# A fused attention and feed-forward block: first token chunks prepared ahead of the branch, the feed-forward part's first work placed in the last KV head's turns

## The chip, the cores and the metric

The kernel runs on one core of a Trainium2 chip. The metric is the device time of one execution in microseconds (us). The core has a matrix engine (TensorE, PE in the profile), a vector engine (VectorE, DVE), an activation engine (ScalarE, ACT), a general engine (GpSimd, POOL) and SyncE (SP), which issues all DMAs here. Each engine executes its own list of instructions in order and waits on semaphores for the others. PEld is the loading of TensorE's weights.

## The reference

The inputs are 2 sequences of 1024 tokens, 512 wide, in float32. First comes an attention with two parts on the same projections, then a gated feed-forward whose weights are rounded to 16 levels (NF4). Both are wrapped in a layer norm before and after:

```python
x = x + layernorm(attn(layernorm(x), Wq, Wk, Wv, Wo))
x = x + layernorm(ffn(layernorm(x), w1, w2, w3))

def attn(h):                       # 32 query heads, 8 KV heads, D = 128, window W = 64
    q, k, v = h @ Wq, h @ Wk, h @ Wv
    g = k
    o_lin = gla_scan(softmax(q), softmax(k), v, log_sigmoid(g) / 16)
    y = sliding_window_attn(rope(q), rope(k), v)
    return bf16(0.5 * y + 0.5 * o_lin) @ Wo

def gla_scan(q, k, v, g):          # per token
    S = S * exp(g)[:, None] + k[:, None] * v[None, :]
    o = q @ S

def ffn(h):                        # 512 -> 1376 -> 512
    a, b, c = nf4(w1), nf4(w2), nf4(w3)      # absmax per 64 values, nearest of 16 codes
    return (silu(h @ a.T) * (h @ b.T)) @ c.T
```

## The kernel before

**Start.** All of `Wk` is loaded in four rows of 128x1024, squared on ScalarE, and summed by TensorE into the column norms (`norms`). From their largest value VectorE makes a flag, `small_gates` (line 1179). Every engine reads it and branches (`tc.If`, line 1181): `fast_attention` where a chunked form of the scan is safe in float32, else `general_attention`. Each is followed by `feed_forward`. These inputs take the fast branch.

**Tokens.** The 2048 tokens are 16 chunks of 128. `input_norms(ci)` loads a chunk into a quantisation tile (tag `zx`), `normed` normalises it on VectorE, with one POOL instruction (`rstd`, line 152, a power) inside it. `input_transposes(ci)` transposes it on TensorE in four 128x128 pieces and ScalarE copies the result into `xnT` (line 303). Four chunks are done ahead of the first turn; the others follow two per turn in turns 0 to 5.

**Turns.** The attention is a list of `N_` = 128 turns, one for each KV head `g`, sequence `b` and chunk `c`; a turn handles the four query heads of its KV head for 128 tokens. The calls of the turn's loop are written out by hand, apart for even and odd turns, and the engines get them in that order (`InOrder`, line 116, so nearly all attention instructions have that line in the profile). A turn works on three stages at once: scores, softmax, linear part and values of turn n; the projection of turn n - 1 by `Wo` (`project`, tile `py`), collected into `yacc` on VectorE; and the query products of turn n + 1. In even turns the key products (`pk`) of the two turns n + 2 and n + 3 are made as well. POOL does the rotary embedding of keys and queries (`rope`: `tmp`, `kr`, `qtmp`, `qr`).

**Weights.** `load_weights(g)` loads `wkv`, `wq` (two buffers each) and `wo` (one). `part_weights` splits `wo` on POOL into a rounded part and a remainder, `wop`, in a format TensorE takes faster: one cast and one subtraction for each of four heads. For head 0 it is called four times ahead of the first turn; for the others in turns 2 to 5 of the second sequence of the head before.

**Quantisation.** The rounding of `w1`, `w2` and `w3` runs as a list of steps (`order`) in all turns from `BEGIN` = 6 on: signs on ScalarE, a multiply-and-maximum chain on VectorE (`zp`, `zm`), six steps in an even turn and three in an odd one. The results go to DRAM (`dq1`, `dq2`, `dq3`).

**Feed-forward.** It begins when the attention's pools are closed. `tokens(x2T, ci)` normalises a chunk of `yacc`, adds the input, stores the sum in `yacc`, normalises again, and transposes into `x2T` (line 1115); `up_weights(f)` loads two rows of `dq1` and `dq2` and transposes them (`tw`, line 1089); `down_weights(f)` the same for `dq3` (line 1098). There are four blocks of 512 tokens and `NFT` = 11 rows of up to 128 hidden values. For every block and row TensorE makes `pgate` and `pup` (line 1136, four products of 128x128x512 each, two passes each), ScalarE the sigmoid (a table of its own), VectorE two multiplications into `hT`; then four output products `pf` per block (line 1154), a layer norm, the sum with `yacc` and the store. In the first block the weights are transposed two rows ahead of their use. A scheduler decides the order of this part's instructions.

## Time and profile before

| | us |
|---|---|
| median of 3 runs | 2175.61 |
| lowest and highest run | 2174.6, 2177.53 |
| profiled execution | 2172.86 |
| its span, first to last instruction | 2171.1 |
| TensorE busy | 2104.6 |
| flag ready on VectorE | 15.97 |
| first key product | 39.30 |
| first scores (`ps`) | 55.90 |
| last projection (`py`) begins | 1666.35 |
| first gate product | 1690.90 |

The mean granted TensorE clock is 0.988. A line of the profile's groups or timeline names line, engine, operation, the written tile, the read tiles, the shape, and how often it stands there; in a timeline the first two numbers are start and duration in us, and the brackets hold the idle time of the engine before it and what ended it. A matmul in float32 shows as two passes, so eight instructions for four products. Matmuls are pipelined: a single one shows as longer than the distance to the next.

### The profile page before, as it was taken

What the parts mean: (1) busy time and instruction counts of PE and PEld (TensorE: products, weight loads), DVE (VectorE), ACT (ScalarE), POOL (GpSimd) and SP (SyncE); (2) the same over time, 40 slices, a digit from 0 to 9 for tenths busy, and PEclk for the clock granted to TensorE, in tenths of its full rate; (3) what the DMA queues carried; (4) which work ended last, traced back from release to release, by engine and by line L of the source; (5) the groups of instructions that cost most, each with busy time, mean ns of one, the idle gap of its engine ahead of it and who ended that gap; (6) DMA issues with size and microseconds to landing.
All of it is one profiled execution on the core that took longest, in us unless ns stands there. A gap on an engine that the chain in (4) does not pass through costs nothing.

```text
span 2171.1 us, 27563 instructions
## 1 busy us (share of the span) xinstructions
PE 2104.6 (97%) x8948; PEld 1409.9 (65%) x8948; DVE 1489.6 (69%) x2822; ACT 1362.9 (63%) x3944; POOL 944.1 (43%) x1290
## 2 busy tenths in 40 slices
PE   4999999999999999999999999999996999999998
PEld 2667777777777777777777777777774544444443
DVE  3668888888788888888888888888887425142222
ACT  2568888888888888888888888888884210101000
POOL 3445555655475556456555655565452101010000
PEclk7999999999999999999999999999998999999999
DMA  5100100010010001000100100000002301000000
GB/s 194 45 15 11 59 11 15 25 49 11 9 58 10 15 15 59 11 10 20 53 11 15 39 33 11 12 11 20 13 6 68 115 27 39 0 29 0 20 0 21
DMA packets 45192, 64.52 MB, mean 30 GB/s; under 512 B 3632, under 2 KB 19632, under 8 KB 45040
## 3 DMA queue, kind: packets, MB, share of 16 engines
q1 hardware_dynamic: 45040, 62.67, 8.8%
q8 instruction: 73, 1.20, 0.2%
q14 instruction: 79, 0.65, 0.1%
HBM read 50.01 MB, written 12.65 MB: 29 GB/s over the span
## 4 chain that ended last, share of the span: by engine, by line
PE 90%; POOL 3%; ACT 2%; DVE 2%; DMA 1%; issue 1%; POOLq 0%; ACTq 0%; SPq 0%; DVEq 0%
PE pq L116 19%; PE py L116 10%; PE pk L116 10%; PE ot L116 9%; PE pgate L1136 7%; PE pf L1154 7%; PE pup L1136 7%; PE pa L116 7%; PE ps L116 5%; PE tr L116 3%; PE tq L116 3%; PE pg L116 2%; POOL qr L116 1%; PE pS L116 1%; PE pt L116 1%; ACT ps L116 1%
## 5 line engine op out<-in xcount | busy, mean ns | idle before, releaser
L116 PE MATMUL pq<-wq,xnT 128*128 128x512 f32 x1024 | 460.6, 592 | 0.0
L116 POOL TENSOR_TENSOR qtmp<-q,fcos 128x512 f32<-128x512 f32 x128 | 162.0, 1266 | 580.3 <-ACT q L116 580.3
L116 PEld LDWEIGHTS pq<-wq,xnT 128*128 128x128 f32 x1024 | 184.9, 190 | 183.7 <-issue 183.6
L116 ACT ACTIVATE zs<-xw,fbounds 128x512 bf16<-128x512 f32 (+3 forms) x416 | 287.8, 723 | 0.0
L116 PE MATMUL py<-wop,oc 128*128 128x512 f32 x1024 | 270.5, 406 | 1.3 <-ACT oc L116 1.3
L152 POOL TENSOR_TENSOR rstd<-ve,mhalf 128x1 f32<-128x1 f32 x64 | 35.7, 565 | 515.0 <-DVE ve L150 499.0
L116 ACT ACTIVATE ps<-ps,nms 128x128 f32<-128x128 f32 x512 | 175.0, 342 | 110.7 <-DVE nms L116 94.7
L116 PE MATMUL pk<-wkv,xnT 128*128 128x256 f32 x1024 | 233.4, 381 | 0.0
L116 ACT ACTIVATE pq<-pq,nmq 128x128 f32<-128x128 f32 x512 | 175.1, 342 | 91.7 <-DVE nmq L116 79.2
L1139 ACT ACTIVATE sg<-pgate 128x512 f32<-128x512 f32 (+1 forms) x44 | 26.2, 597 | 324.9 <-PE pgate L1136 324.9
L116 PEld LDWEIGHTS pk<-wkv,xnT 128*128 128x128 f32 x1024 | 195.9, 191 | 47.0 <-issue 14.1
L116 PEld LDWEIGHTS py<-wop,oc 128*128 128x128 f32 x1024 | 182.9, 189 | 36.6 <-ACT oc L116 1.7
L116 POOL TENSOR_TENSOR qr<-q,fsin 128x256 f32<-128x256 f32 x256 | 206.0, 825 | 0.0
L116 DVE SCALAR_TENSOR_TENSOR zp<-zp,zs 128x512 f32<-128x512 f32 (+3 forms) x224 | 195.4, 872 | 9.4 <-ACT zs L116 5.0
L116 POOL TENSOR_TENSOR qr<-qr,qtmp 128x512 f32<-128x512 f32 x128 | 165.8, 1295 | 9.8
L116 DVE SCALAR_TENSOR_TENSOR zm<-zm,zs 128x512 f32<-128x512 f32 (+3 forms) x192 | 163.0, 849 | 5.7 <-ACT zs L116 3.0
L1136 PE MATMUL pgate<-x2T,w1T 128*128 128x512 f32 (+1 forms) x352 | 160.4, 594 | 0.0
L1136 PE MATMUL pup<-x2T,w2T 128*128 128x512 f32 (+1 forms) x352 | 158.2, 592 | 0.0
L116 DVE TENSOR_TENSOR ps<-ps,fwin 128x512 f32<-128x512 f32 x128 | 89.2, 697 | 96.3 <-PE ps L116 95.4
L1154 PE MATMUL pf<-w3T,hT 128*128 128x512 f32 (+1 forms) x352 | 151.8, 592 | 0.0
L116 PE MATMUL ps<-kT,qrT 128*128 128x128 f32 x1024 | 136.5, 276 | 0.2
L116 DVE TENSOR_REDUCE nmq<-pq 128x4 f32<-128x512 f32 x128 | 87.8, 686 | 59.4 <-ACT q L116 59.4
(125 smaller groups left out, 4078.9 us busy)
## 6 DMA issues: line engine op xcount, KB each, us to landing
wq<-in_L_attn_Wq_dram SPq DMA_DIRECT2D x8, 1024.0 KB, 6.1
wo<-in_L_attn_Wo_dram SPq DMA_DIRECT2D x8, 1024.0 KB, 5.1
xw<-in_L_ffn_w_dram SPq DMA_DIRECT2D x20, 256.0 KB, 2.6
dq<-zp SPq DMA_DIRECT2D x20, 256.0 KB, 2.0
row<-dq SPq DMA_DIRECT2D x20, 256.0 KB, 2.8
x<-_attn_hidden_states_dram SPq DMA_DIRECT2D x16, 256.0 KB, 2.7
xc<-_attn_hidden_states_dram SPq DMA_DIRECT2D x16, 256.0 KB, 2.6
out_dram<-res SPq DMA_DIRECT2D x16, 256.0 KB, 2.0
```

The source lines that it names most:

```text
L116: return lambda *args, **kwargs: self.tc.keep_in_program_order(getattr(self.engine, name)(*args, **kwargs))
L152: nc.gpsimd.tensor_tensor(rstd, ve, mhalf, ALU.pow)
L1136: nc.tensor.matmul(pg[:n, :], lhsT=wT[:, kt, f * P : f * P + n], rhs=x2T[:, kt, :], start=kt == 0, stop=kt == KT - 1)
L1139: nc.scalar.activation(sg[:n, :], ps[0][:n, :], AF.Sigmoid)
L1154: nc.tensor.matmul(pf, lhsT=hT[:n, f, m * P : (m + 1) * P], rhs=w3T[:n, f, :], start=f == 0, stop=f == NFT - 1)
```

## The change

1. **Ahead of the branch.** `xnT`, `wkvs`, `wqs`, `wos` and the rotary `tables` are tiles of the whole kernel now. The part before the branch loads chunks 0 and 1 between rows 1 and 2 of `Wk`, chunks 2 and 3 after row 3, then head 0's `wkv`, `wq` and the tables; it normalises, transposes and copies the four chunks (`AHEAD` = 4) in a fixed order between the squares and the flag. Chunk 3 is normalised after the flag.
2. **Other chunks.** They are staged in a buffer of the `wop` tile, normalised in place, two in turns 0 and 1 and one a turn after that, in turns 2 to 9. `wo` of head 0 is loaded after the branch, and its parts are made after the first softmax transposes (two heads) and at the end of turn 0 (two heads). Quantisation begins with turn 2.
3. **Last KV head (turns 112 to 127).** `feed_forward_begun(n)` runs at the end of every turn. From turn 116 on it loads the first rows of the up weights, from turn 117 to 124 it transposes eight of them, one a turn; in turns 117, 119, 121, 123 it does the first half of a token chunk (`tokens`), in 118, 120, 122, 124 the second normalisation, in 119, 121, 123, 125 the transposes. Turn 126 makes the gate product of row 0, turn 127 the up product of row 0 and the gate product of row 1, and the up product of row 1 lies ahead of the last projection.
4. **Tiles.** The feed-forward part has no pools of its own: its weights, hidden values and work tiles lie in `wqs`, `wkvs`, `wos`, `tables`, the `wop` buffers, `xnT` and, after the last turn, the attention's tiles; PSUM is that of the attention. All its TensorE, VectorE and ScalarE instructions are kept in program order.

The diff, cut to its core (the general branch and the plain feed-forward that follows it are left out):

```diff
-            for ci in range(2 * CB):
-                input_norms(ci)
-                input_transposes(ci)
-            weights = {0: load_weights(0)}
+            def all_weights(g):
+                return *load_weights(g), parts_tile(f"wop{g}"), load_out_weights(g)
+            for ci in range(AHEAD, AHEAD + 2):
+                chunk_loaded(staged(ci), ci)
...
+            weights = {0: (*first_weights, parts_tile("wop0"), load_out_weights(0))}
             qb = load_const("fbounds", [P, 16], F32, con["bounds"])
+            for ci in range(AHEAD + 2, AHEAD + 2 * GRP):
+                chunk_loaded(staged(ci), ci)
...
-            for h in range(GRP):
-                part_weights(0, h)
             key_products(0)
...
             softmax_transposes(0)
-
-            BEGIN = (NCI - 2 * CB) // 2
+            for h in range(2):
+                part_weights(0, h)
+            arriving = iter(range(AHEAD, NCI))
+            BEGIN = 2
+            L = N_ - NB * NCH
+            F = FeedForward((pmm, "mm"), (psc, "sc"), (ptr, "tr"), (po, "o"))
...
+            def feed_forward_begun(n):
+                if n == L + 2:
+                    up = quarters(parts_tile("wup"))
+                    for f in range(4):
+                        F.w1[f], F.w2[f] = up[:, f, :], up[:, 4 + f, :]
+                    F.xc, F.yn, F.xn, F.sg = ([wqs[0][:, j, :]] for j in range(4))
+                    F.rows = [wos[:, j, :] for j in range(4)]
...
+                k = n - (L + 5)
+                if 0 <= k < 8:
+                    F.up_weights(k % 2, k // 2, early["row", k])
+                if -1 <= k < 7:
+                    early["row", k + 1] = F.load_up((k + 1) % 2, (k + 1) // 2)
+                if k >= 2 and k % 2 == 0 and k // 2 - 1 < F.MB:
+                    F.token_transposes(k // 2 - 1, early["xn"])
+                if k >= 0 and k // 2 < F.MB:
+                    if k % 2 == 0:
+                        F.tokens(k // 2, early["xc"])
+                    else:
+                        early["xn"] = F.token_norms(k // 2)
+                if k >= -1 and k % 2 and (k + 1) // 2 < F.MB:
+                    early["xc"] = F.load_tokens((k + 1) // 2)
...
-                inputs = list(range(2 * CB + 2 * n, min(2 * CB + 2 * n + 2, NCI)))
+                inputs = list(islice(arriving, 2 if n < 2 else 1))
...
                     if keys2:
                         key_products(n + CB)
+                    else:
+                        gate0 = F.up_product(0, 0, 0)
...
+                    if n == 0:
+                        for h in range(2, GRP):
+                            part_weights(0, h)
                 else:
+                    if not more:
+                        up0 = F.up_product(1, 0, 0, "gate")
                     score_softmax(n)
+                    if not more:
+                        F.hidden(0, gate0, up0, F.sigmoid(0, gate0))
...
+                    else:
+                        gate1 = F.up_product(0, 0, 1)
+                        sg1 = F.sigmoid(1, gate1)
                     values(n)
...
             rounded_heads(N_ - 1)
+            up1 = F.up_product(1, 0, 1)
             project(N_ - 1)
+            F.hidden(1, gate1, up1, sg1)
             collect(N_ - 1)
...
+            F.run(2, 4)
...
+    class FeedForward:
...
+        def token_norms(self, ci):
+            xn = self.next("xn")
+            normed(xn, yacc[:, ci, :], self.vector)
+            return xn
...
+        def run(self, f0, ready):
...
+                for f in range(f0 if tb == 0 else 0, NFT):
+                    gate = self.up_product(0, tb, f)
+                    sg = self.sigmoid(f, gate)
+                    if row:
+                        self.up_weights(0, row[0], row[1][0])
+                    if tb == 0:
+                        col = next_down(col)
+                    up = self.up_product(1, tb, f)
+                    if row:
+                        self.up_weights(1, row[0], row[1][1])
+                        row = loaded_up(next(ups, None))
+                    self.hidden(f, gate, up, sg)
...
         for kt in range(KT):
             nc.sync.dma_start(wka[:, kt, :], wk[kt * P : (kt + 1) * P, :])
-            nc.scalar.activation(wka[:, kt, :], wka[:, kt, :], AF.Square)
+            if kt % 2:
+                for ci in (kt - 1, kt):
+                    chunk_loaded(chunks[ci], ci)
+        first_weights = load_weights(0)
+        load_tables("fcos", "fsin")
...
+        for ci in range(2):
+            normed(chunks[ci], chunks[ci], vector)
+        squares(0)
+        squares(1)
+        transposed(0)
+        squares(2)
+        transposed(1)
+        squares(3)
+        normed(chunks[2], chunks[2], vector)
...
+        normed(chunks[3], chunks[3], vector)
+        transposed(2)
+        transposed(3)
     flag = nc.values_load(small_gates, min_val=0, max_val=1, skip_runtime_bounds_check_because="the result of a comparison")
```

## The prediction

> **What bounds the kernel now.** I read the page first (busy shares, then the 40 slices), then TensorE's waits, busy time by stage, and last the instructions in order of time at both ends of the attention.
>
> ```profile
> span 2171.1 us, 27563 instructions
> ...
> PE 2104.6 (97%) x8948; PEld 1409.9 (65%) x8948; DVE 1489.6 (69%) x2822; ACT 1362.9 (63%) x3944; POOL 944.1 (43%) x1290
> ...
> PE   4999999999999999999999999999996999999998
> ...
> PEclk7999999999999999999999999999998999999999
> ```
>
> TensorE is the bound, and it stands still in three places only: the first slice, slice 31, and the tail. The stages show how much:
>
> ```profile
> 16.00:22.30 6.30, 0.00 (x0) 0.00 (x0) 2.40 (x8) 0.00 (x0) 1.73 (x4) 0.76 0.69 228
> 22.30:39.30 17.00, 3.91 (x16) 3.19 (x17) 6.08 (x11) 1.75 (x3) 8.47 (x10) 0.50 0.79 245
> 39.30:44.90 5.60, 5.60 (x18) 4.59 (x18) 1.46 (x4) 0.60 (x2) 0.55 (x1) 0.65 0.92 283
> 44.90:55.90 11.00, 6.81 (x25) 3.88 (x23) 6.11 (x17) 6.45 (x22) 9.11 (x18) 0.89 0.49 166
> 55.90:70.20 14.30, 13.34 (x64) 9.86 (x64) 7.09 (x15) 7.89 (x27) 7.79 (x13) 0.97 0.06 21
> ...
> 1650.10:1668.50 18.40, 13.54 (x65) 9.69 (x64) 10.48 (x17) 7.04 (x22) 3.59 (x4) 1.00 0.03 12
> 1668.50:1687.30 18.80, 3.29 (x12) 2.15 (x12) 14.54 (x38) 1.75 (x3) 4.66 (x8) 0.58 0.61 196
> 1687.30:1698.80 11.50, 11.46 (x38) 6.88 (x39) 9.96 (x24) 4.81 (x7) 2.33 (x4) 0.80 0.51 156
> 1698.80:2163.00 464.20, 464.20 (x1205) 211.96 (x1203) 134.10 (x256) 42.13 (x73) 18.80 (x34) 1.00 0.08 24
> ```
>
> Columns: stretch, length, busy time of PE, PEld, DVE, ACT, POOL, granted clock, DMA. From 16 to 39 us TensorE does 3.9 us of work; from 1668.5 to 1687.3 it does 3.3 us at clock 0.58. After 1698.8 it never waits, so nothing there can be gained. In order of time, the start:
>
> ```profile
> 5.67 8.70 PE L1173 MATMUL norms<-wka,ones 128*1 128x512 f32 x16 [5.67 <-ACT wka L1171]
> ...
> 19.17 0.48 SPq L312 DMA_DIRECT2D wo<-in_L_attn_Wo_dram  x1
> ...
> 29.36 0.61 POOL L116 CAST wop<-wo 128x512 fp32r<-128x512 f32 x1 [7.13 <-DMA wo<-in_L_attn_Wo_dram]
> ...
> 39.30 5.55 PE L116 MATMUL pk<-wkv,xnT 128*128 128x256 f32 x16
> ...
> 52.74 0.58 PE L116 MATMUL pt<-ident,kh 128*128 128x128 f32 x2 [3.81 <-DVE kh L116]
> ```
>
> The flag is ready at 15.97, SP issues at 16.68, and the first key product waits until 39.30.
>
> **Part 1, the start.** *Ahead of the branch.* The four rows of Wk land 1.26 us apart (512 KB each). Two token chunks (256 KB, 0.63 each) now lie before rows 2 and 3, which land near 8.2 and 9.5. The new order ties ScalarE to TensorE: the square of row 2 stands behind the copy of chunk 0's transposes, the square of row 3 behind chunk 1's. TensorE begins at 5.67 with passes 0.86 apart for 3.8 us, then 0.43: rows 0 and 1 to 10.8, transposes 0.44; copy 0.58 and square 1.06 to 13.0; four passes 1.72, transposes, copy, square to 16.95; last passes to 18.8 (14.37 before). Reductions 1.6: flag at 20.7, 4.7 later. Chunk 3 is normalised after that (DVE 0.69+0.18+0.14, POOL 0.55, DVE 0.55, with gaps 2.3) and TensorE transposes it before its own branch: 23.5. With the 0.7 that SP's branch took, the first key product starts at 24.3 instead of 39.3: 15.0 gained. No row shows a branch with the DMA queues full; between 0.7 again and a DMA's landing (2.7) on top, I take 0.7, SP's row.
>
> [...]
>
> *Chunk 0's chain.* TensorE has then been idle 3.8 us, so I leave the key product its 5.55 (after the 3.81 us wait above, four transposes took 1.09 to 1.12 against 0.60 at full clock). [...] Now the parts of Wo: before, POOL made all of them from 29.36 to 37.99, under the wait for tokens. Now wo is issued after the branch, behind two chunks and three constants (near 26.5; it lands after 5.1 at the median, 32), and POOL's order has cast 0.61, subtract 1.26, cast 0.61 between chunk 0's key rope (done near 33.7) and query rope, and another 1.26 inside it: 3.7 on the path. The rope's transposes come at 41.7 (53.52 before, 11.8 gained). VectorE has chunk 6's normalisation, waiting for POOL, before qs: scores(0) at 44.8 against 55.90, 11.1 gained.
>
> *Turns 0 to 9.* The statistics and normalisations of chunks 7 and 8 stand before the mask of turn 0, each waiting for POOL, which is making the last two parts: mask 2.2 late, and scores(1) at about 61.8 against 70.16, 8.4 gained. From scores(1) to scores(10) before took 121.7; work is four pairs of 25.18 (the spacing of 1607.48 and 1632.66), a turn of 11.4 and ten transposes of 0.44, 116.5. Part of the 5.2 between is the second chunk of a turn, whose transposes wait for the first one's copy:
>
> ```profile
> PE xtp L116 <- ACT xnT L303: 4.0, 6, 0.7
> ```
>
> Now only turns 0 and 1 have two chunks: I give back 3.0. Quantisation starts four turns earlier, where the input norms were; its work per turn is that of the steady turns, 0.2 us of idle in 50: nothing. **Start: 11.4 gained**; ends 4 (branch fetch, later wo) and 17 (15.0 with warm clock, no rope delay).
>
> **Part 2, the transition.** From 1650.1 to 1698.84 is 48.7 us. Work at full clock in it: the attention's rest 12.0, 16 token and 16 weight transposes 3.5, two products of 3.44: 22.4. So 26.3 are lost. Now four token chunks and eight weight tiles lie in turns 117 to 125, the four products of the first two rows in turns 126 and 127. In turn 127 by rows: scores 0.9, up product 3.44, linear 1.7 end at +6.1, while mask, maximum, exponentials, sw end at +5.4; the sigmoid's table load (1.28) lies beside that, hT at +7.9, A at +8.6 under the projection (to +8.4) and gate product (to +11.8); values, then up product 3.44 over the heads' two copies (1.24). Nothing waits. Before, this stretch waited for S 2.3, sw 0.7, oc 1.3.
>
> *What it costs.* Each token chunk adds two normalisations of 2.1 in order on VectorE, with a POOL round trip inside. The even turn's end has no room, the odd one's 1.6:
>
> ```profile
> 1594.81 0.70 DVE L116 TENSOR_TENSOR ps<-ps,fwin 128x512 f32<-128x512 f32 x1 [1.59 <-PE ps L116]
> ...
> 1607.73 0.76 DVE L116 SCALAR_TENSOR_TENSOR zp<-zm,zp 128x576 f32<-128x576 f32 x1
> ...
> 1608.58 0.70 DVE L116 TENSOR_TENSOR ps<-ps,fwin 128x512 f32<-128x512 f32 x1
> ```
>
> The first line is an odd turn's successor, the last an even one's: its mask starts as the quantisation step ends. So `token_norms` at the even ends makes the next mask late by 2.1 less one weight transpose, 1.6, and odd turns have nothing to spare (rope's transposes wait for POOL by 0.2 to 0.5 there): 1.6 in turns 119 and 121, 0.8 in the two after, where quantisation runs out (its 544 steps at nine a pair from turn 2 end at 122.9). `tokens` at the odd ends costs 0.9, inside the even turn's 2.8 between sw (ended 1600.42) and mix (1603.22). Where a turn has both a weight and a token transpose, three times, the second waits 0.68: 2.0. ScalarE's three copies a pair (1.8) fit its idle 4.6 of 25; without that the exponentials would be late by as much. SP's row and token loads are issued turns ahead, so a 2.8 landing is hidden; late, they would hold TensorE by what is missing. **Six lost** in all; ends 2 (all cover holds) and 15 (every one of eight token steps stops TensorE for its 2.1).
>
> **Part 3, the rest.** First two rows aside, the feed-forward keeps its products, transposes and copies, now in program order on TensorE, VectorE and ScalarE. Product pairs of 6.9 us cover a transpose's copy (0.59 to 0.69) and the loads (2.8 to 3.2) one row ahead: nothing; ends 0 and 5 (0.1 a row over 44). The tail's last normalisation and store stay.
>
> **Sum.** 2172.86 - 11.4 - 26.3 + 6.0 = 2141.2 against the profiled execution (span 2171.1 and 1.8 around it). The median of the runs, 2175.61, lies 2.75 higher, so 2144.
>
> **Rivals.**
> 1. *More of the start is gained.* POOL gets wo late enough to do query rope first, and TensorE stays warm: 17 at the start, 2 lost in the turns: 2172.86 - 17 - 26.3 + 2 + 2.75 = 2134. For it: 15.0 is gained up to the first product. Against: POOL's order is fixed, and 3.81 idle did cool the clock.
> 2. *The engines of the last head have no room,* or the start is given back by wo: 15 lost in the turns gives 2153; only 4 gained at the start gives 2151. For it: VectorE is busy 82 to 85 us in 100 there. Against: after turn 122 quantisation is gone.
> 3. *The work is not really woven in:* a load or a reused tile makes the transposes wait until the attention is over. Then the 26.3 stay, 2172.86 - 11.4 + 2.75 = 2164. Against: tiles of the seventh head's weights are free from turn 112, and row loads need only the first two dequantised matrices (374 of 544 steps, done by turn 86).
> 4. *Slower: the last head's turns fall to half clock.* One mechanism, in turns 117 to 127: token steps in VectorE's queue stop TensorE for over 3.8 us a turn, after which it runs its first 3.8 us at half rate (1.9 lost), 5.7 a turn, 63 in eleven: 2172.86 - 11.4 - 26.3 + 63 + 2.75 = 2201. It decides from 37.7 / 11 = 3.4 lost a turn. My steps give at most 1.6; TensorE's 2.31 wait in turn 127 of before did not cool it.
>
> **How the numbers follow.** Forecast (2137 to 2150) 0.56; rival 1 (2129 to 2137) 0.17; rival 2 (2150 to 2160) 0.19; rival 3 0.04; rival 4 0.04. The range 2131 to 2158 leaves out rivals 3 and 4 and the outer ends of 1 and 2, about 0.15. A change under 0.2% (4.4 us) can't be told from none on this kernel: slower 0.04, same 0.01, faster 0.95.
>
> **What would show it.** After: the flag near 20.7 and the first key product near 24; the rope's first transposes ended by POOL's query rope with a wop operation inside it; scores(1) near 62; from turn 117 small waits of TensorE, in odd turns for VectorE's sw or POOL's rope and for ScalarE's copies at the second transposes; no wait over 2 us between the last scores and the first gate product of row 2, with a granted clock of 1.00 throughout; feed-forward turns as before. Wrong would be: a first key product after 28 or before 20, a wait over 3 us in the last head, or a TensorE busy time that grew by more than the clock's share.

## The result and the profile after

The changed kernel takes 2147.59 us (median of 4 runs, 2147.42 to 2148.68) against 2176.26 us (4 runs, 2174.6 to 2177.53) for the kernel before on the same chip: a ratio of 0.9874, 95% interval 0.9862 to 0.9887, 28.7 us faster. The forecast was 2144 with a range of 2131 to 2158. The profiled execution took 2147.43 us, 25.4 less than the one of before; its span, busy times, slices of TensorE and granted clock from the page:

```profile
span 2145.6 us, 27553 instructions
...
PE 2103.7 (98%) x8948; PEld 1409.7 (66%) x8948; DVE 1492.3 (70%) x2822; ACT 1359.7 (63%) x3944; POOL 944.6 (44%) x1290
...
PE   6899999999999999999999999999999999999998
...
PEclk8999999999999999999999999999999999999999
```

The slice that held the transition (slice 31, a 6 before) is full, and the first one holds more (6 instead of 4); the second holds a little less (8 instead of 9). The same 8948 matmuls and nearly the same busy time (2104.6 before) fill a span 25.5 us shorter: the change removed standing still, not work. Busy time by stage (stretch, length, busy time and instructions of PE, PEld, DVE, ACT, POOL, granted clock, DMA share, GB/s):

```profile
0.00:23.90 23.90, 11.67 (x32) 3.23 (x33) 7.52 (x19) 7.06 (x8) 2.98 (x12) 0.97 0.73 241
...
28.60:44.80 16.20, 7.46 (x24) 4.01 (x24) 7.62 (x23) 6.55 (x22) 14.61 (x24) 0.73 0.89 301
44.80:65.00 20.20, 16.84 (x65) 11.99 (x64) 10.78 (x24) 7.84 (x27) 12.28 (x19) 0.79 0.16 55
65.00:78.70 13.70, 12.67 (x66) 9.05 (x65) 8.91 (x23) 8.49 (x27) 6.04 (x9) 1.00 0.12 36
78.70:96.40 17.70, 15.83 (x71) 11.53 (x70) 11.85 (x29) 10.63 (x33) 9.20 (x13) 0.94 0.09 30
1526.70:1663.90 137.20, 132.44 (x639) 95.34 (x638) 102.56 (x206) 94.53 (x290) 65.28 (x94) 1.00 0.09 28
1663.90:2145.60 481.70, 473.61 (x1236) 218.06 (x1234) 156.97 (x297) 45.74 (x83) 21.90 (x40) 1.00 0.08 25
```

The stretches end at marks: first key product 23.9, scores of turn 0 at 44.8, of turn 1 at 65.0, turn 2 at 78.7, turn 3 at 96.4, turn 117 at 1526.7, turn 127 at 1663.9. From there TensorE works until the last normalisation and store. In the start 8.7 us still pass without work between the first key product's end and scores(0), and then, in turn 0, at clock 0.79, 3.4 more; turn 2 loses 1.9.

Comparing the start of each turn's scores with before tells where the gain lies:

| turn's scores | before | after | earlier by |
|---|---|---|---|
| 0 | 55.90 | 44.83 | 11.07 |
| 1 | 70.16 | 64.98 | 5.18 |
| 2 | 83.71 | 78.71 | 5.00 |
| 3 | 99.42 | 96.36 | 3.06 |
| 6 | 141.68 | 134.85 | 6.83 |
| 10 | 191.88 | 186.54 | 5.34 |
| 117 | 1532.48 | 1526.70 | 5.78 |
| 127 | 1656.09 | 1663.86 | -7.77 |
| end | 2171.1 | 2145.6 | 25.5 |

The start is worth 5.3 us, not the 11.4 forecast. Turns 117 to 127 take 137.16 us against 123.61, 13.55 more. 8.7 of it is work that was moved there (eight weight and four token transposes of 0.44, one product of 3.44); the other 4.8 are what waits cost. These are all the waits there (what TensorE waited for in the stretch from 1526 to 1670; total, times, longest):

```profile
PE ptr L118 <- ACT wup L118: 2.0, 3, 0.7
PE pa L118 <- DVE S L118: 1.5, 2, 0.8
PE tr L118 <- POOL qr L118: 0.9, 2, 0.5
PE pa L118 <- DVE sw L118: 0.4, 2, 0.2
```

They too sum to 4.8, but that is partly chance. Before, the same turns held 1.2 us of waits, so by the brackets only 3.6 are new; and the stop in turn 119 cost more than its bracket says: the product behind the wait of 0.82 starts 1.42 after the one ahead of it, where the same two lie 0.43 apart in the kernel before, so that it lost 0.99.

From scores(127) to the end it takes 481.7 instead of 515.0. The 33.3 less, minus the 8.7 of work that left, are 24.6 gained, so that the transition as a whole gives 24.6 - 4.8 = 19.8 (forecast: 26.3 - 6.0 = 20.3). Its heart is turn 127, in order of time:

```profile
1663.86 1.06 PE L118 MATMUL ps<-kT,qrT 128*128 128x128 f32 x8
1664.75 3.60 PE L118 MATMUL pgate<-xnT,wup 128*128 128x512 f32 x8
1668.19 0.59 PE L118 MATMUL pa<-qh,kT 128*128 128x256 f32 x2
...
1672.22 3.59 PE L118 MATMUL pgate<-xnT,wup 128*128 128x512 f32 x8
```

(The products of the feed-forward part carry the names pgate and pup by turns; the trace names a buffer, not its use.) No line has a bracket with a wait: the product of 3.44 lies where before TensorE waited 2.3 for the state S, the next stands between projection and values.

### The profile page after: what moved, and what is told of

Read it like the earlier page. It is cut to its first block, busy times and chain, and to the rows that moved or that the text cites. A ratio compares the mean times of both kernels' runs of the same rounds, so it can differ in the third digit from the quotient of the medians.

```text
span 2145.6 us, 27553 instructions
## 1 busy us (share of the span) xinstructions
PE 2103.7 (98%) x8948; PEld 1409.7 (66%) x8948; DVE 1492.3 (70%) x2822; ACT 1359.7 (63%) x3944; POOL 944.6 (44%) x1290
## 4 chain that ended last, share of the span: by engine, by line
PE 87%; ACT 4%; DVE 4%; POOL 3%; issue 1%; DMA 0%; ACTq 0%; POOLq 0%; DVEq 0%
PE pq L118 18%; PE py L118 9%; PE ot L118 9%; PE pk L118 9%; PE pgate L118 7%; PE pout L118 7%; PE pup L118 7%; PE pa L118 7%; PE ps L118 5%; PE tr L118 3%; PE tq L118 2%; PE pg L118 2%; POOL qr L118 2%; ACT ps L118 1%; PE pt L118 1%; PE pS L118 1%
## 5 line engine op out<-in xcount | busy, mean ns | idle before, releaser
L118 POOL TENSOR_TENSOR qtmp<-q,tables 128x512 f32<-128x512 f32 x128 | 162.2, 1268 | 586.8 <-ACT q L118 586.6
L118 POOL TENSOR_TENSOR qr<-q,tables 128x256 f32<-128x256 f32 x256 | 206.2, 826 | 0.0
L118 PEld LDWEIGHTS ps<-kT,qrT 128*128 128x128 f32 x1024 | 126.1, 194 | 0.9 <-ACT qrT L118 0.6
L118 ACT ACTIVATE ffqrT<-pgate 128x512 f32<-128x512 f32 (+1 forms) x21 | 12.5, 597 | 176.3 <-PE pgate L118 176.3
L118 PE MATMUL ot<-qh,S 128*128 128x512 f32 x224 | 114.4, 592 | 0.0
L118 ACT ACTIVATE wq<-pgate 128x512 f32<-128x512 f32 (+1 forms) x23 | 13.7, 597 | 153.1 <-PE pgate L118 153.1
```

What stands on the lines that cost most here:

```text
L118: return lambda *args, **kwargs: self.tc.keep_in_program_order(getattr(self.engine, name)(*args, **kwargs))
```

## The experiments

Each edit is made to the changed kernel, alone where nothing else is said. The medians stand beside its 2147.59 us, and beside 2174.6 to 2176.0 for the kernel before, which ran on the same chip as each. That kernel's own median thus moves by 1.4 us, so a difference of one or two us between medians says little by itself; there the traces have to decide.

### 1. The weave taken out, and the start undone

First the weave: the first tokens, weights and products of the feed-forward part stand behind the attention again.

```diff
-                if 0 <= k < 8:
-                    F.up_weights(k % 2, k // 2, early["row", k])
...
-                    if k % 2 == 0:
-                        F.tokens(k // 2, early["xc"])
-                    else:
-                        early["xn"] = F.token_norms(k // 2)
...
-                        gate0 = F.up_product(0, 0, 0)
...
-                        up0 = F.up_product(1, 0, 0, "gate")
...
-                        gate1 = F.up_product(0, 0, 1)
...
-            up1 = F.up_product(1, 0, 1)
...
-            F.run(2, 4)
+            for ci in range(F.MB):
+                F.tokens(ci, F.load_tokens(ci))
+                F.token_transposes(ci, F.token_norms(ci))
+            for f in range(2):
+                for i in range(2):
+                    F.up_weights(i, f, F.load_up(i, f))
+            F.run(0, 2)
```

> The start stays as in the changed kernel; the feed-forward part's first tokens, its first rows' weights and their four products follow the attention again. Theory (the weave is worth the 26.3 us of waits lost after the last turn, less the waits it puts into turns 117 to 127, 4.8 by the trace of the changed kernel; about 20 in all): 2147.6 + 20 = 2167 to 2169, turns 117 to 127 back from 137.2 to about 124 us, and TensorE standing still for over 20 us after the last turn. Rival (part of the 28.7 us gained in all is the start's, more than the 5.3 that the turns show): the weave is worth 14 or less, 2162 or below.

Measured: 2172.13 us (10 runs, 2169.7 to 2174.54; ratio to before 0.9985, 0.9976 to 0.9995); the profiled execution's span is 2167.6, 22.0 longer than the changed kernel's. Scores(117) come at 1526.63, the same as with the weave; turns 117 to 127 take 122.68, and then TensorE waits four times, here the first three (start, duration, instruction, wait ahead of it in brackets):

```profile
1667.77 1.11 PE L118 MATMUL ptr<-ident,wq 128*128 128x128 f32 x4 [6.07 <-DVE wq L118]
1673.06 1.11 PE L118 MATMUL ptr<-ident,wq 128*128 128x128 f32 x4 [4.17 <-DVE wq L118]
1678.57 1.09 PE L118 MATMUL ptr<-ident,wq 128*128 128x128 f32 x4 [4.39 <-DVE wq L118]
```

Each token chunk's second normalisation is waited for by itself, 19.0 us in four waits; written one after the other, these steps make the rest after scores(127) 3.3 longer than in the kernel before (518.3 against 515.0). Taking off these 3.3 and adding the 0.9 by which turns 117 to 127 are shorter than before, the 22.0 become 19.6. By the traces, then, the weave is worth about 20 us against the old kernel, as the theory has it, and the rival's 14 or less is out. The theory's time was too low: 2172.13 lies above its 2167 to 2169. The 3.3 of this edit were not in it, and the medians lie 24.5 apart, 2.5 more than the profiled executions (the profiled one was the fastest of the ten); no trace shows where these 2.5 lie.

Then the start: the first four chunks, weights and tables behind the branch, Wo's parts ahead of the first key product.

```diff
-            for ci in range(AHEAD, AHEAD + 2):
+            for ci in range(AHEAD):
                 chunk_loaded(staged(ci), ci)
+            for ci in range(AHEAD):
+                input_norms(ci)
+                input_transposes(ci)
+            first_weights = load_weights(0)
+            first_out = load_out_weights(0)
+            load_tables("fcos", "fsin")
...
+            for h in range(GRP):
+                part_weights(0, h)
             key_products(0)
...
-        for ci in range(2):
-            normed(chunks[ci], chunks[ci], vector)
-        squares(0)
-        squares(1)
-        transposed(0)
...
+        for kt in range(KT):
+            squares(kt)
```

> Chunks 0 to 3, the first head's weights and the tables are loaded, normalised and transposed after the branch again, and Wo's parts are made before the first key product; the weave stays. Theory (the start has kept 5.3 of the 15.4 us by which its first key product is earlier): 2147.6 + 5.3 = 2153, scores(0) near 56 and scores(2) near 84. Rival (the start is worth the 11.4 forecast and the rest is lost somewhere else): 2159.

Measured: 2150.09 us (2148.23 to 2151.72), ratio to before 0.9881 (0.9865 to 0.9898), 2.5 us slower than the changed kernel. TensorE at the start:

```profile
25.17 3.79 PE L118 MATMUL xtp<-ident,tokens 128*128 128x128 f32 x16 [10.31 <-DMA wkv<-in_L_attn_Wv_dram]
28.76 4.58 PE L118 MATMUL pk<-wkv,xnT 128*128 128x256 f32 x16
```

The first key product comes at 28.76 although the chunks are loaded after the branch: 10.5 earlier than the 39.30 of before, in which the four chunks went through two buffers and their second pair was loaded behind Wo. So the changed queue of loads behind the branch gives two thirds of the 15.4 us, and preparing ahead of the branch 4.8. Scores(0) were expected near 56 and came at 47.24; scores(10) at 190.47, 3.9 later than in the changed kernel. What this edit takes back is 3.9 in the trace and 2.5 in the medians, less than the theory's 5.3; the rival's 11.4 is out. It is not the price of the branch alone: all of Wo's parts stand ahead of the key rope on POOL here, which starts at 38.08.

### 2. Where the missing six microseconds went

Three candidates at the start: Wo's parts on POOL; normalisations that VectorE takes early; the squares ahead of the branch. POOL in the changed kernel, in order of time:

```profile
39.40 1.25 POOL L118 TENSOR_TENSOR wop<-wos,wop 128x512 fp32r<-128x512 f32 x1
40.62 1.25 POOL L118 TENSOR_TENSOR qr<-qr,qtmp 128x512 f32<-128x512 f32 x1
...
47.32 0.72 POOL L161 TENSOR_TENSOR rstd<-ve,mhalf 128x1 f32<-128x1 f32 x1
...
56.15 1.26 POOL L118 TENSOR_TENSOR qr<-qr,qtmp 128x512 f32<-128x512 f32 x1
57.37 0.55 POOL L161 TENSOR_TENSOR rstd<-ve,mhalf 128x1 f32<-128x1 f32 x1
```

and VectorE:

```profile
48.08 0.55 DVE L166 TENSOR_SCALAR tokens<-tokens,mv,rstd 128x512 f32<-128x512 f32 x1 [0.35 <-POOL rstd L161]
48.66 0.70 DVE L118 TENSOR_TENSOR ps<-ps,fwin 128x512 f32<-128x512 f32 x1
...
57.95 0.94 DVE L166 TENSOR_SCALAR tokens<-tokens,mv,rstd 128x512 f32<-128x512 f32 x1 [2.96 <-POOL rstd L161]
...
59.01 0.69 DVE L118 TENSOR_TENSOR qs<-pq,rsq 128x512 f32<-128x512 f32 x1
```

Between the two halves of the query rope stands a subtraction of Wo's parts (39.40). In turn 0 the reciprocal roots (rstd) of later chunks come out of POOL behind further parts (47.32) and behind the next query rope (57.37). VectorE has the normalisations that need them ahead of the mask (48.08, then 48.66) and of the normalised queries (57.95, after 2.96 us of standing still, then 59.01). TensorE's transposes of these queries wait 1.72.

*Normalisations in program order.*

```diff
-    normed(staged(ci), staged(ci))
+    normed(staged(ci), staged(ci), vector)
```

> The later token chunks' normalisations stand in VectorE's queue in program order, in their turns, where the changed kernel lets them be moved up; on POOL that puts the query rope of chunk 0 ahead of Wo's parts. Theory (the 6 us missing at the start went to normalisations that VectorE took early and that waited for POOL, which was making Wo's parts): rope's transposes near 38.5 instead of 41.9, scores(0) near 41.5 instead of 44.8, turn 0 at most 17 us instead of 20.2, turn 2 at most 16; 2142 to 2144. Rival (in order, each normalisation of about 2.1 us stops the next mask, in some twelve turns): scores(0) earlier as well, but turns 2 to 9 longer by 1 us each; 2148 to 2155.

Measured: 2150.38 us (2149.89 to 2151.31), slower than the changed kernel by 2.8. The theory came true up to scores(0): rope's transposes at 37.57, scores(0) at 39.45, 5.4 earlier (forecast 41.5). Turns 0 and 2 got shorter, but not by as much as it said (17.64 and 16.72, at most 17 and 16 forecast). Then the rival came true: turns 1 to 9 take 132.7 us where the changed kernel takes 121.6, and scores(10) come at 189.75, 3.2 later than there. The waits of TensorE that are new (turns 0 to 9):

```profile
PE ot L118 <- DVE A L118: 7.3, 5, 2.3
PE xtp L118 <- DVE tokens L118: 6.5, 7, 1.6
```

They sum to 13.8 us in twelve places, 10.3 of them in turns 1 to 9. The early place of the normalisations is therefore no fault by itself; it loses up to the end of turn 0 and in turn 2, and pays in the other turns up to 9.

*Only chunks 4 and 5 in program order.*

```diff
-    normed(staged(ci), staged(ci))
+    normed(staged(ci), staged(ci), *((vector,) if ci < 6 else ()))
```

> Only chunks 4 and 5, those of turn 0, are normalised in program order; all later chunks as in the changed kernel. Theory B (what the start lost is the normalisations taken early, ahead of the work of turn 0; what order costs comes in the turns after it, 1.6 to 3 each): scores(0) near 39.5, scores(1) near 57, and from turn 2 on the intervals of the changed kernel (17.7 for turn 2 at most, 14.2 and 11.7 then), so 4 to 6 kept; 2142 to 2144. Rival (the chunks that are still free are moved up all the same and wait for POOL there, so that turn 1 takes what turn 0 gives back): scores(3) less than 2 earlier; 2146 to 2148.

Measured: 2143.84 us (2142.84 to 2144.23), 3.8 faster than the changed kernel. Scores(0) at 39.76, scores(1) at 57.96, scores(10) at 182.17, 4.4 earlier. Theory B's time came, its course not wholly: turn 1 took 15.96 instead of 13.73 and turn 2 18.10, because the freed chunks were moved up into turn 1, where the mask stood behind two of them.

*Wo loaded later and its parts written later*, first together, then each alone.

```diff
-            weights = {0: (*first_weights, parts_tile("wop0"), load_out_weights(0))}
...
             for ci in range(AHEAD + 2, AHEAD + 2 * GRP):
                 chunk_loaded(staged(ci), ci)
+            weights = {0: (*first_weights, parts_tile("wop0"), load_out_weights(0))}
...
-            for h in range(2):
-                part_weights(0, h)
...
-                        for h in range(2, GRP):
+                        for h in range(GRP):
                             part_weights(0, h)
```

The first two signs are the load's place, the others the parts'.

> Wo of the first head is loaded behind the six further token chunks, and its four parts are made at the end of turn 0, so that POOL makes chunk 0's query rope without them. Theory A (the parts inside the rope are what the start lost): rope's transposes near 38.3 instead of 41.9, scores(0) near 41.3 and all later turns 3 earlier; 2144. Theory B (the normalisations that VectorE took early are what it lost; the run with them in order gained 5.4 at scores(0) and 4.8 at scores(2)): scores(0) 2 to 3 earlier, but the token chunks' normalisations still stand ahead of the mask of turn 0 and of its normalised queries, so that less than 1.5 is left at scores(2); 2146 to 2148.

> Of the two edits of the run with Wo late, only the load: Wo of the first head is issued behind chunks 6 to 11; its parts stay where the changed kernel writes them. Theory (the place of the load does it: the token chunks land about 3 us earlier, and POOL, whose order follows what has landed, makes the reciprocal roots and the rope before the parts): 2142 to 2143.5, turn 0 near 16 us. Rival (it was the parts written behind turn 0): 2147.

> The other edit alone: all four parts of Wo are written at the end of turn 0, the load stays where the changed kernel has it, ahead of chunks 6 to 11. Theory (the load's place does it, and two casts and two subtractions still stand inside chunk 0's rope because Wo has landed by then): rope's transposes near 42, scores(0) near 45, 2147. Rival (it was the parts' place): 2142 to 2143.5.

| run | median us | rope's transposes | scores(0) | turn 0 | scores(10) |
|---|---|---|---|---|---|
| changed kernel | 2147.59 | 41.92 | 44.83 | 20.15 | 186.54 |
| both | 2142.74 | 39.70 | 43.98 | 15.90 | 181.06 |
| load later | 2142.83 | 40.39 | 44.68 | 15.65 | 181.89 |
| parts later | 2146.55 | 42.29 | 48.42 | 16.11 | 185.71 |

The load alone gives the whole 4.8 us (4.7 at scores(10) in the traces); the parts' place alone gives 1.0 (0.8 there). Theory A had the time of the first run right and the place wrong: rope's transposes came 2.2 earlier, but scores(0) only 0.9, since the transposes of the normalised queries then waited 2.29 for VectorE's statistics. The gain is in turn 0, as neither text said: 4.3 of the 5.5 us. With the load later, POOL and VectorE read:

```profile
39.07 1.27 POOL L118 TENSOR_TENSOR qr<-qr,qtmp 128x512 f32<-128x512 f32 x1
...
42.16 0.61 POOL L118 CAST wop<-wos 128x512 fp32r<-128x512 f32 x1
...
50.02 1.16 POOL L161 TENSOR_TENSOR rstd<-ve,mhalf 128x1 f32<-128x1 f32 x2
```

```profile
46.63 0.70 DVE L118 TENSOR_TENSOR ps<-ps,fwin 128x512 f32<-128x512 f32 x1 [1.91 <-PE ps L118]
...
54.63 0.69 DVE L118 TENSOR_TENSOR qs<-pq,rsq 128x512 f32<-128x512 f32 x1
```

POOL did not get these instructions in the order of the program text, in which the parts stand behind chunk 0's rope in both kernels (their calls go through `InOrder` too); the build placed them, and the load's place changed where: with it moved, the rope runs without a part inside, and the parts start at 42.16. The six token chunks were issued from 27.58 to 30.35 (27.55 to 31.70 with Wo's 1 MB ahead of them), so that most of them are normalised before scores(0), and only two roots are left for turn 0 (50.02). The mask comes 1.95 after scores(0) instead of 3.83 and then waits for nothing but TensorE; the normalised queries come 2.1 after sw (52.54), 4.7 in the changed kernel. That is 1.9 and 2.6, together the 4.5 by which turn 0 is shorter. In the run with the parts later and the load early, TensorE waited 4.1 us ahead of scores(0) instead, for VectorE, which stood 6.4 for POOL: the wait moved, the time hardly did. What the load's place does through POOL's order and what through the chunks' earlier landing, the runs do not separate.

*The squares first.*

```diff
-        for ci in range(2):
+        for ci in range(AHEAD):
             normed(chunks[ci], chunks[ci], vector)
-        squares(0)
-        squares(1)
-        transposed(0)
-        squares(2)
-        transposed(1)
-        squares(3)
-        normed(chunks[2], chunks[2], vector)
+        for kt in range(KT):
+            squares(kt)
+        for ci in range(AHEAD):
+            transposed(ci)
...
-        normed(chunks[3], chunks[3], vector)
-        transposed(2)
-        transposed(3)
```

> Ahead of the branch the squares of all four rows of Wk come before the transposes of the four token chunks, so that ScalarE's squares no longer stand behind copies. Theory (what is gained before the branch is kept): flag near 17 instead of 20.4, first key product near 20, 4 earlier; scores(0) and all later turns 3 to 4 earlier; 2144. Rival (turns 0 and 2 are set by POOL and by Wo's arrival and not by the first key product): scores(0) earlier by 2 or less, scores(10) by less than 1; 2147 to 2148.

Measured: 2141.77 us (2140.59 to 2142.15), 5.8 faster than the changed kernel. The flag is ready at 16.85 (20.56), the first key product comes at 17.84 (23.92), scores(0) at 38.14, scores(10) at 180.67: the last three 6.1, 6.7, 5.9 earlier. What is gained ahead of the branch is kept in full, and the rival's numbers are out. Its mechanism is not: Wo is issued behind the branch, so its load came earlier too (20.12 instead of 26.50), and turn 0 took 19.99, as long as in the changed kernel. The order that ties ScalarE's squares to the copies of the transposes costs about 6 us.

### 3. Turn 2

In every other run turn 2 took 16.7 to 18.5 us, while the next even turn with a chunk takes 14.2 (15.4 with all normalisations in order). VectorE in turn 2 of the changed kernel:

```profile
83.31 0.68 DVE L118 TENSOR_REDUCE zam<-xw 128x8 f32<-128x512 f32 x1
...
88.84 0.55 DVE L166 TENSOR_SCALAR tokens<-tokens,mv,rstd 128x512 f32<-128x512 f32 x1 [2.54 <-POOL rstd L161]
...
89.54 0.69 DVE L118 TENSOR_TENSOR xw<-xw,zrb 128x512 f32<-128x512 f32 x1
...
91.13 0.68 DVE L118 TENSOR_TENSOR qs<-pq,rsq 128x512 f32<-128x512 f32 x1
```

The lines of xw and zam are the first steps of the quantisation of the feed-forward weights, which now begins in turn 2 (in turn 6 before). After the reduction zam the variance of a token chunk (ve) is ready at 84.91, and its root comes out of POOL only behind the whole query rope. POOL in turn 2:

```profile
84.33 1.26 POOL L118 TENSOR_TENSOR qtmp<-q,tables 128x512 f32<-128x512 f32 x1 [8.24 <-ACT q L118]
...
87.04 1.27 POOL L118 TENSOR_TENSOR qr<-qr,qtmp 128x512 f32<-128x512 f32 x1
88.26 0.55 POOL L161 TENSOR_TENSOR rstd<-ve,mhalf 128x1 f32<-128x1 f32 x1
```

One constant was changed:

```diff
-            BEGIN = 2
+            BEGIN = 4
```

> The changed kernel with one constant different: the quantisation of the feed-forward weights begins in turn 4 and not in turn 2. Theory (turn 2 takes 17.7 us, about 3 more than a turn with one chunk, because the first steps of quantisation stand ahead of the normalised queries and of A there): turn 2 at most 15, turn 4 of its usual 14.2 or at most 1 above it, 2144 to 2146. Rival 1 (where quantisation begins, its first steps cost these 3 us in any turn): turn 4 near 17, 2147. Rival 2 (turn 2 is long because a token chunk's normalisation waits for POOL there): turn 2 above 16.5, 2147 to 2149.

Measured: 2148.36 us (2147.91 to 2149.2), no faster. Turn 2 took 14.21 and turn 4 14.21, as the theory said; scores(10) at 182.69, 3.9 earlier, and the lead is still 3.4 at turn 117. Then it is given back: the quantisation, started two turns later, runs on two turns further into the last head, and turns 117 to 127 take 139.15 instead of 137.16, with a third wait each for S and sw. The last product ends 1.4 earlier than in the changed kernel's profile, and 2.1 more pass until the profile's last instruction, for which nothing in the trace shows a cause. POOL in turn 2 of this run:

```profile
83.87 1.17 POOL L161 TENSOR_TENSOR rstd<-ve,mhalf 128x1 f32<-128x1 f32 x2 [7.45 <-DVE mv L157]
84.90 1.27 POOL L118 TENSOR_TENSOR qtmp<-q,tables 128x512 f32<-128x512 f32 x1
```

The variances are ready before the rope, the roots stand ahead of it, and VectorE waits 0.4 instead of 2.5. In turn 4, where the quantisation now begins, there is no token chunk left to normalise. So by the traces turn 2 lost most to one reduction that made a root miss its place in POOL's queue, a meeting of two streams; the theory's own cause is there as well, but smaller (the step xw, 0.69 at 89.54, stands ahead of the normalised queries). Rival 1 falls with turn 4, rival 2 with turn 2, which has its normalisation still. But of the 3.4 that a later start of the quantisation brings to turn 117, 2.0 go in the last head, and the rest in the unexplained 2.1 at the end.

### 4. The token steps the other way round

```diff
-                k = n - (L + 5)
+                k = n - (L + 4)
```

> In turns 118 to 125 the two token steps change places: the first normalisation of a feed-forward token chunk at the ends of the even turns, the second with its transposes at the ends of the odd turns; the same work. Forecast's pricing (a normalisation pair of about 2.1 us at an even end makes the next mask 1.6 late, and odd turns have nothing to spare, the wait for S in turns 119 and 121 being its result): the waits for S go at 119 and 121, but odd ends lose as much; turns 117 to 127 take 137 again, 2147 to 2149. Rival (odd ends have room for it): the 0.8, 0.2, 0.5 and 0.7 us waits of turns 119 and 121 go, 135 or less; 2144 to 2145.5.

The edit moves every step of the early feed-forward work one turn ahead, the weight transposes too (turns 116 to 123), and the token transposes stand at the ends of the even turns now, not of the odd ones as the expectation has it.

Measured: 2149.41 us (2148.07 to 2150.57). Turns 117 to 127 take 137.34 instead of 137.16, and with turn 116, in which the first steps now lie, it is 151.54 instead of 150.93: no less than in the changed kernel, with one wait of 0.8 for S instead of two, but three for POOL's rope instead of two and 2.8 instead of 2.0 for the second transposes. The forecast's pricing holds, odd ends have no more room. (1.2 of the 1.7 us by which this profile is longer arose in turns 0 to 9, in which the order of the instructions is the same as in the changed kernel on TensorE, VectorE, ScalarE and POOL: that much one profile can differ from another. Here 0.9 of it is turn 1, with a granted clock of 0.91 where the changed kernel's profile has 1.00.)

### 5. Together

The squares first (2141.77 alone) and Wo loaded and split later (2142.74 alone); in a second run chunks 4 and 5 in program order as well (2143.84 alone). The diff against the run with the squares first:

```diff
-            weights = {0: (*first_weights, parts_tile("wop0"), load_out_weights(0))}
             for ci in range(AHEAD + 2, AHEAD + 2 * GRP):
                 chunk_loaded(staged(ci), ci)
+            weights = {0: (*first_weights, parts_tile("wop0"), load_out_weights(0))}
...
-                        for h in range(2, GRP):
+                        for h in range(GRP):
                             part_weights(0, h)
```

> Both together: the squares of all four rows of Wk before the transposes of the token chunks, and Wo of the first head loaded and split behind chunk 0's query rope. Theory (the two gains, 5.8 and 4.9 by the medians of the single runs, are separate: one moves the flag, the other the work between the first key product and turn 1): 2147.6 - 10.7 = 2137, scores(0) near 37.5, scores(1) near 53.5. Rival (with the flag 6 earlier the token chunks and tables arrive later than the work asks for them, and one gain hides the other): 2140 to 2142.

> As the run before it, with chunks 4 and 5 normalised in program order too. Theory (Wo's parts and the early normalisations are two links of one chain, part, reciprocal root on POOL, normalisation, mask, so that taking away the second adds little once the first is gone): scores(1) within 2 us of the run before, and 2135.5 to 2139. Rival (two separate causes, 4.9 and 3.8 by the medians of the single runs): 2133.

The first two together: 2135.84 us (2135.41 to 2136.15), ratio to before 0.9822 (0.9805 to 0.9838), 11.8 faster than the changed kernel and 39.7 faster than the one before. The sum of the single gains was 10.7. Page and TensorE:

```profile
span 2133.6 us, 27554 instructions
...
PE 2097.3 (98%) x8948; PEld 1405.8 (66%) x8948; DVE 1491.5 (70%) x2822; ACT 1359.3 (64%) x3944; POOL 944.1 (44%) x1290
```

```profile
17.88 3.69 PE L118 MATMUL pk<-wkv,xnT 128*128 128x256 f32 x16 [1.21 <-DVE small_gates L118]
...
53.60 1.06 PE L118 MATMUL ps<-kT,qrT 128*128 128x128 f32 x8
```

Turn 0 takes 15.89 and turn 2 17.24, as in the run with Wo late; the flag's gain lies ahead of them. With the third edit on top it is 2140.08 us (2139.42 to 2140.67), 4.2 slower: scores(0) come at 31.20 and scores(1) at 50.45, 6.5 and 3.2 earlier than without it, but turn 1 takes 20.03 instead of 13.74 and turn 2 18.47 instead of 17.24. Neither text had that. The theory (one chain, little added) is wrong at scores(0), and the rival (two separate gains) at the end: what the edit gains up to turn 0 it loses in turn 1, where VectorE stood 1.46 and 1.49 for POOL, which was making Wo's parts there, with mask and S behind.

## Why the prediction was right, and where it was not

*Ahead of the branch.* Right to a few tenths: flag ready at 20.56 (20.7 forecast), first key product 23.92 (24.3). The flag's own terms, 18.8 and 1.6, add up to 20.4 and not to 20.7; the last passes ended at 18.97 and the reductions took 1.59. The key product lasted 4.66, not 5.55, at a mean granted clock of 0.79; the warm clock in the start's upper end of 17 is what the combined run shows, 3.69 for the same product. The branch fetch in the lower end of 4, and a DMA's landing on top of the 0.7, no run shows: in the changed kernel the trace has no idle time ahead of the first key product, in the run with the squares first 0.33 us of issue stood there, and in the combined one it began 1.0 after the flag was ready at 16.89.

*Chunk 0's chain.* Right, with the place: a cast, a subtraction and a cast before the rope, a subtraction inside it; rope's transposes at 41.92 (41.7), scores(0) at 44.83 (44.8).

*Turns 0 to 9.* This step failed, by 6.1 us (11.4 forecast, 5.3 measured), in two terms:
- Turn 0 was put at 17.0 and took 20.15. The mask was priced 2.2 late for Wo's parts, and it was about 1.9 late. What the step did not price is the same queue a second time: a reciprocal root behind chunk 1's query rope on POOL, VectorE waiting 2.96 for it ahead of the normalised queries, and the clock at 0.79 for the turn. The step also took the place of Wo's load as given where it was the cause; issuing that load seven places later gives 4.8.
- "I give back 3.0" in turns 1 to 9 gave 0.2. To price "Quantisation starts four turns earlier" at nothing was the mistake: beginning it in turn 2 cost that turn 3.4 us (17.65 against 14.21 when it starts later). A mean idle time per steady turn says nothing on the turn in which a new stream begins beside work that isn't steady yet.

*Part 2.* 19.8 gained, 20.3 forecast, closer than its two terms: 24.6 came where 26.3 were forecast (the 26.3 are counted from 1650.1, and 1.0 of them lies ahead of scores(127), in turn 126), and the waits cost 4.8 where 6.0 were forecast. The waits came for the causes named: 1.5 in turn 119 and 1.3 in turn 121 (S and sw at VectorE, POOL's rope; forecast 1.6 each), 2.0 for three second transposes (forecast 2.0). Only the 0.8 put on the two turns after did not come. Turn 127 waits for nothing, the clock is 1.00.

*Part 3.* Nothing, as forecast: outside the last normalisation TensorE never waits after scores(127).

*Sum.* Forecast 2141.2 for the profiled execution against 2147.43: 6.2 too low, the start's error. The 2.75 between median and profiled execution of before, added to it, is 0.16 in the changed kernel; so the forecast of the median is off by 3.6 only because two errors partly cancelled, which is luck.

*Rivals.* 1, more gained at the start: not in this kernel, but its mechanism is real; with Wo landing late enough for the rope to go first, 2142.8; with the squares first as well, 2135.8, beside its 2134, and 17.2 gained at scores(10), beside its 17 at the start. 2: its second arm, the start given back by Wo (2151, 4 gained), was the nearest to what happened at the start, with the last head as forecast. 3: out, the weave alone is worth 20. 4: out; the longest wait in the last head is 0.8, the clock stays at 1.00.

## What to carry to other kernels

A load's place in the queue can be worth more than the work it feeds: with Wo issued ahead of six token chunks, POOL had Wo's parts ahead of the rope and of reciprocal roots, VectorE waited for those roots, and TensorE's first turn for VectorE; one moved line gave 4.8 us back. When a change brings a start forward, follow the gain turn by turn until the pace is steady, and price every stream that starts earlier with it in its first turn, not by the steady mean. Two gains add only if they cut different chains: squares first and Wo later did (5.8 and 4.9 alone, 11.8 together); ordering the first normalisations, worth 3.8 alone, on top took 4.2 away.

## What the runs showed of the hardware

The clock fell after waits of 0.76 and 0.87 us in one place and stayed at 1.00 after one of 2.31 in another. In turn 2 of the changed kernel TensorE was busy 0.24, 0.53 and 0.60 of three successive microseconds (two waits of 0.76 and 0.87, and short gaps), and the granted clock then was 0.57, 0.50, 0.50 and 0.72 in the four microseconds from 94 to 98 (stretch, length, busy times of PE, PEld, DVE, ACT, POOL, clock, DMA share, GB/s):

```profile
91.00:92.00 1.00, 0.24 (x3) 0.13 (x2) 1.00 (x3) 1.00 (x2) 0.00 (x0) 1.00 0.00 0
92.00:93.00 1.00, 0.53 (x4) 0.29 (x4) 1.00 (x3) 0.28 (x2) 0.85 (x2) 1.00 0.00 0
93.00:94.00 1.00, 0.60 (x3) 0.55 (x4) 0.35 (x1) 0.97 (x5) 0.92 (x3) 1.00 0.00 0
...
95.00:96.00 1.00, 0.76 (x4) 0.55 (x4) 1.00 (x3) 1.00 (x3) 1.00 (x2) 0.50 0.00 0
```

The same place reads nearly the same in three other runs (no weave, load later, token steps the other way round): waits of 0.76 and of 0.87 or 0.88, after which the next scores took 1.59 to 1.64 us (1.64 in the changed kernel, 1.06 a turn earlier in all four). In turn 127 of the kernel before, a wait of 2.31 made three successive microseconds emptier still, and the clock stayed at 1.00 until after the last projection:

```profile
1657.00:1658.00 1.00, 0.15 (x2) 0.00 (x0) 0.78 (x2) 0.32 (x1) 0.00 (x0) 1.00 0.00 0
1658.00:1659.00 1.00, 0.00 (x0) 0.00 (x0) 1.00 (x2) 0.29 (x2) 0.00 (x0) 1.00 0.00 0
1659.00:1660.00 1.00, 0.54 (x3) 0.49 (x4) 0.75 (x3) 0.94 (x6) 0.00 (x0) 1.00 0.00 0
```

No single wait was longer than 2.31 us in the two places, and the clock fell in the one whose longest wait was 0.87. Neither the longest wait nor the busy share of three microseconds tells the two apart; what decides stays open.
